# Two of seven block products taken in seven again: a dense graph-layer kernel on one core, with PSUM banks shared anew and a new written order

## The chip, the cores and the metric

The kernel runs on one core of a Trainium2 chip. The metric is the device time of one execution in microseconds (us); before the change its median over 3 runs is 2155.39 us (2154.95 to 2155.68).

## The reference, cut to what matters

Four layers work on x, 128 graphs of 128 nodes with 512 features, in fp32. Each layer adds its result to x and takes a layernorm over the features (no scale, no shift).

```python
# layer 0
y = einsum('nm,bmd->bnd', adj, x);  out = einsum('bnd,do->bno', y, weight) + bias
# layer 1
q = x @ Wq.T;  k = x @ Wk.T;  v = x @ Wv.T
rel = adj.T * (q @ k.T);  rel = rel / norm(rel, axis=2);  out = rel @ v
# layer 2
h = x @ W;  e = leaky_relu(h @ a1 [:, None] + h @ a2 [None, :], 0.2) * adj
out = elu(softmax(e) @ h + beta * h)
# layer 3
A = adj @ x;  C = A + b;  out = max over features of relu(A + (C - A))   # per node
x = layernorm(x + out)   # after each layer
```

The kernel uses that layer 1's scores are x (Wq.T Wk) x.T, that layer 2's aggregation can come before the weight product ((att + beta I) x) W, and that layer 3's sum is A + b.

## The kernel before, in words

The 128 graphs are worked in 32 groups of 4 (`G`, `NG`), so a group is 512 rows. Per group there are four big products of 512 x 512 by 512 x 512, named after their weight: `y` with weight "0" (layer 0), `m` with "m" (x times the combined Wq.T Wk, made once in the fill as product `qk`), `v` with "v", and `z` with "2" (layer 2). Besides these there are, for each of the 4 graphs, small PE pieces: the aggregation `p_y` (with adj), the scores `p_rel`, the attention times values `p_o`, the aggregation `p_z`, and `p_a` of layer 3.

**Seven products.** Each big product is split into 2 x 2 blocks of 256 and taken in Strassen-Winograd form: seven block products instead of eight (`product`, L451), on sums and differences of the weight's blocks (`weight_blocks`, L157, made once) and of the left factor's blocks (`left_factors`, L335, by GpSimd, for every product). A block product is four fp32 matmuls of 128 x 128 weights with 256 columns. They accumulate in three PSUM regions (`REGION`, L332): region 0 collects products 1, 6, 7 and 4, region 1 product 2, region 2 products 5 and 3. After each product, what the region holds by then is brought into its output block (`BLOCK`, L333) by a ScalarE copy or a VectorE addition (`out`, L481). In y the bias is laid into the regions beforehand by ScalarE (`fill`, L457).

In the steady groups (y of groups 2 to 31, m and v of 1 to 30, z of 0 to 29), product 2, which feeds only block (0, 0), is itself taken in seven products of 128-blocks (`inner_product`, L420): its own sums of the left factor are made by GpSimd (`inner_sums`, L354, 128 columns wide), its own sums of the weight once (`inner`, L183), and its seven 128 x 128 x 128 products come in four stretches (`SMALL`, L400) that share one PSUM bank with tag "pi" and are added to the four quarters of the output block by VectorE, seven additions of 128 columns.

**The written order.** Nothing is scheduled by a planner. Every piece of work is put into a list by `emit` with a number, its place in the order (L240); `TABLE` (L252) holds the places for a group, and group g is shifted by 28 g. The list is sorted and emitted (L1141), and each engine works through its own pieces in just that order (`InOrder`, L18). A group spans some 110 units, so four groups are in work at once, each in another layer; a period of 28 units has one group's worth of every piece. Inside a big product the places are in `STEPS` (L408): for each block product when it starts and when its output is taken, and likewise for the inner stretches. `EARLY` and `FIRST` (L273, L281) hold the places of groups 0 and 1, `LAST` (L289) those of the last three groups. In the fill the order of the products is y of group 0, qk, m of group 0, y of group 1, v of group 0; these are plain (all seven products of 256-blocks, in the order 1, 2, 6, 5, 7, 3, 4).

**Between the layers.** VectorE adds residuals, takes the dots of layer 2 (`dots`, L739), the statistics and the row maxima; ScalarE copies products out of PSUM, squares, exponentiates and applies the normalisations (`apply`); GpSimd makes the left sums and every -1/2 power of a layernorm (`norm`, L522). Transposes of x and of the attention go through VectorE in blocks of 32 and then DMA (`turn_blocks`, `move`), issued from SyncE.

**PSUM.** The eight banks are: two for all small PE pieces (tag "ps", `bank`, L85), two for region 0 ("r0"), one for regions 1 and 2 ("r12"), one for the inner products ("pi"), and two for the constant vectors of layer 2 ("wa").

```python
ORDER = (1, 2, 6, 5, 7, 3, 4)
REGION = {1: 0, 6: 0, 7: 0, 4: 0, 2: 1, 5: 2, 3: 2}
BLOCK = {1: (0, 0), 2: (0, 0), 6: (0, 1), 3: (0, 1), 5: (1, 1), 7: (1, 1), 4: (1, 0)}
```

Of the kernel before, what the change touches and what calls it, by code (L numbers as in the profile page):

```python
# [8 lines left out]
FP = mybir.dt.float32  # L9
AF = mybir.ActivationFunctionType  # L10
ALU = mybir.AluOpType
# [18 lines left out]
def kernel(  # L30
# [41 lines left out]
    G = 4  # L72
# [7 lines left out]
    small = ctx.enter_context(tc.tile_pool(name="small", bufs=4))  # L80
# [51 lines left out]
    for tag, n in (("r0", 2), ("r12", 1)):  # L132
        for i in range(n):
            r = psum.tile([P, 2, H], FP, tag=tag, name=f"first_{tag}_{i}", bufs=n)
            pe.matmul(r, ident, ident[:, None, :].to_broadcast([P, G, P]), start=True, stop=True)
# [21 lines left out]
    def weight_blocks(at, key, w, keep=0, tag=None):  # L157

# [7 lines left out]
        def factor(i):  # L166
            if i == 0:
                home, args = (const, {}) if tag is None else (data, dict(tag=tag))
                u = home.tile([P, 3 + keep, 2, H], FP, name=f"t_{key}", **args)
                t.update({2: u[:, 0], 3: u[:, 1], 4: u[:, 2]})  # L170
                t[1] = u[:, 3] if keep else blk(0, 1)
                bw[key] = {
                    1: blk(0, 0), 2: blk(1, 0), 3: blk(1, 1), 4: t[4], 5: t[1], 6: t[2], 7: t[3],
                }
# [8 lines left out]
        def inner():  # L183

            b = blk(1, 0)
            quad = {(k, c): b[:, k, c * P : (c + 1) * P] for k in range(2) for c in range(2)}
            v = const.tile([P, 4, P], FP, name=f"u_{key}")
# [5 lines left out]
            bw_inner[key] = {  # L193
# [5 lines left out]
        if tag is None:  # L199
            emit(at[3], inner)  # L200
# [46 lines left out]
    def row(at, step, n=G):  # L247
# [3 lines left out]
    YS = 1.3  # L251
    TABLE = dict(  # L252
        load=[-20], y=[0.74, 1.12, 3.36, 3.74], y_sums=[4.5, 5.0, 5.5, 8.0], y_w=row(6.66, 1, 7),
        stats0=[13.7, 14.05, 14.4, 14.7], norm0=[15.15], apply0=row(15.9, 0.33),
        turn=row(21.4, 1), turn_blocks=row(17.3, 0.5),
        move=row(19.3, 0.1), x_sums=row(25.3, 0.5), m=row(28, 1, 7),
        scores=[35.4, 35.78, 38.02, 38.4],
        masked=[38.85], squares=[39.2], turn_rel=[39.1],
        move_rel=row(39.8, 0.1), inverse=[41.0], v=row(41.3, 1, 7),
        attend=[51.12, 52.43, 53.65, 54.02],  # L260
        residual=[51.45, 52.8, 54.0, 54.4], squares1=[51.85, 53.2, 54.35, 54.8],
        dots=[51.75, 53.1, 54.6, 55.6], norm1=[55.9], scale=[57.2],
        apply1=row(65.4, 0.33),
        spread=[57.3], leaky=[61.3], weighted=[62.6], greatest=[63.2], exps=[63.25],
        divide=[64.6], turn_att=[68.6], with_beta=[69.0], turn_blocks_2=[64.95], move_2=[65.0],
        gather=[70.04, 70.42, 72.66, 73.04],
        z_sums=row(73.9, 0.5), z_w=row(76.69, 1, 7), exp=[84.1, 84.9, 96.0, 99.2],
        elu=[85.9, 86.7, 96.85, 99.9], norm2=[101.3], apply2=row(102.3, 0.33),
        widen=[103.95, 104.32, 105.43, 105.81], top=[104.4, 104.95, 105.85, 106.3],
        norm3=[107.3], apply3=row(108.45, 0.33), store=[109.9],  # L270
    )

    EARLY = dict(  # L273
        y=row(0.5, 1), y_sums=row(4.3, 0.5), y_w=row(7, 1, 7),
        stats0=row(14.4, 0.4), norm0=[16.2], m=row(28, 1, 7), scores=row(36.5, 1),
        masked=[39.95], squares=[40.4], turn_rel=[40.3], move_rel=row(41.2, 0.1),
        v=row(42, 1, 7), attend=row(50.6, 1), residual=row(51.0, 1), squares1=row(51.4, 1),
        norm1=[55.5],
# [3 lines left out]
        0: dict(EARLY, stats0=row(15.8, 0.02), norm0=[15.95], apply0=row(18.0, 0.1), turn=row(20.4, 0.3),  # L282
                dots=[57.8, 58.75, 59.9, 60.6], scale=[61.2], spread=[62.0], leaky=[62.3], weighted=[62.9],
                greatest=[64.0], exps=[64.05], divide=[65.05], turn_blocks_2=[65.6], move_2=[65.65]),
        1: dict(y=row(-9.5, 0.3), y_sums=row(-4.0, 0.1), y_w=row(7, 1, 7), stats0=row(14.4, 0.4), norm0=[16.2], attend=[49.7, 52.43, 53.65, 54.02], apply0=row(18.0, 0.1), turn=row(20.3, 0.3),
                x_sums=row(22.5, 0.5)),
# [4 lines left out]
            exp=[0.8, 10.5, 13.0, 18.0], elu=[4.4, 12.3, 17.2, 20.9], norm2=[23.3],  # L291
            apply2=row(24.6, 0.8), squares3=row(28.0, 0.8), widen=[44.7, 54.9, 55.0, 59.3],
            top=[45.6, 58.77, 58.78, 61.05], norm3=[64.32], apply3=row(66.0, 0.8), store=[69.0],
        ),
        NG - 2: dict(
            scale=[4.2], apply1=row(4.5, 0.9), spread=[6.9], leaky=[7.4], weighted=[9.0],
            greatest=[11.5], exps=[12.2], divide=[14.6], turn_att=[18.35], with_beta=[19.6],
            gather=row(33.1, 0.9), z_sums=row(37.0, 0.05),
            z_w=[37.2, 38.9, 41.0, 42.7, 44.9, 46.6, 48.3], exp=[50.3, 51.0, 53.0, 57.0],
            elu=[51.95, 54.2, 58.8, 64.35], norm2=[66.6], apply2=row(67.9, 0.8),  # L300
            widen=[69.3, 70.2, 74.5, 77.3], top=[74.3, 74.9, 76.2, 77.7], stats3=row(75.7, 0.05),
            norm3=[75.95], apply3=row(79.0, 0.8), store=[82.0],
        ),
        NG - 1: dict(
            m=[0.0, 1.73, 3.46, 5.2, 7.4, 9.1, 10.8], scores=row(12.7, 0.9), masked=[16.4],
            squares=[17.2], turn_rel=[20.3], inverse=[19.0],
            v=[16.7, 18.4, 20.6, 22.3, 24.0, 25.8, 27.5],
            attend=row(29.4, 0.86), residual=row(30.4, 0.87), stats1=row(33.9, 0.1),
            norm1=[34.3], dots=row(34.4, 0.1), scale=[42.7], apply1=row(39.0, 0.8),
            spread=[44.0], leaky=[44.1], weighted=[45.6],  # L310
            greatest=[47.0], exps=row(48.0, 0.6), divide=row(48.7, 0.6),
            turn_att=row(49.2, 0.6), with_beta=row(49.7, 0.6), gather=[50.0, 50.9, 55.2, 59.6],
            z_w=[51.8, 56.1, 60.4, 63.9], exp=[55.3, 59.6, 63.9, 67.5],
            elu=[56.5, 62.0, 67.5, 70.9], norm2=[58.75, 64.3, 69.8, 73.2],
            apply2=[60.2, 65.8, 71.3, 74.7], widen=[67.45, 68.4, 73.4, 76.0],
            stats3=[61.1, 66.65, 74.1, 76.5], norm3=[62.0, 67.45, 74.2, 76.6],
            top=[69.86, 73.25, 75.5, 77.0],
            apply3=[70.9, 74.3, 76.4, 78.0], store=[71.8, 75.2, 77.3, 78.9],
# [16 lines left out]
    def left_factors(at, s, aT, tag, name, keep, inner=0):  # L335
# [18 lines left out]
        def inner_sums():  # L354

            a = {
                (j, k): s[aT][:, 2 + k, j * P : (j + 1) * P] for j in range(2) for k in range(2)
            }
            v = work.tile([P, 4, P], FP, tag=tag + "i", name=f"si_{name}")
            s1, s2, s3, s4 = (v[:, i] for i in range(4))  # L360
            pool.tensor_tensor(s1, a[1, 0], a[1, 1], ALU.add)
            pool.tensor_tensor(s2, s1, a[0, 0], ALU.subtract)
            pool.tensor_tensor(s3, a[0, 0], a[1, 0], ALU.subtract)
            pool.tensor_tensor(s4, a[0, 1], s2, ALU.subtract)
            s["fi"] = {1: a[0, 0], 2: a[0, 1], 3: s4, 4: a[1, 1], 5: s1, 6: s2, 7: s3}

        if inner:
            emit(at[2] + inner, inner_sums)
# [14 lines left out]
    def by_columns(p, a, b, first):  # L383

        for c in range(2):
# [15 lines left out]
        ((1, 2), (((0, 0), 1), ((0, 0), 0))),  # L401
        ((6, 5), (((1, 1), 2), ((0, 1), 0))),
        ((7,), (((1, 1), 0),)),
        ((4, 3), (((0, 1), 2), ((1, 0), 0))),
    )


    STEPS = {  # L408
        key: (
            {1: (0.0, 0.45), 6: (1.69, 2.4), 5: (2.62, 3.3), 7: (4.22, 4.9), 3: (5.16, 5.85), 4: (5.91, 6.6)},  # L410
            ((1.5, 1.65), (2.43, 2.6), (4.12, 4.18), (4.97, 5.15)),
        )
        for key in ("m", "0", "v")
    }
    STEPS["2"] = (
        {1: (0.0, 0.6), 6: (1.69, 2.4), 5: (3.0, 3.7), 7: (4.21, 4.9), 3: (5.9, 6.55), 4: (6.64, 7.3)},
        ((1.5, 1.7), (2.81, 2.97), (4.11, 4.2), (5.71, 5.88)),
    )

    def inner_product(at, name, mul, s, w, c):  # L420
# [4 lines left out]
        def step(n):  # L425
            if n == 0:
                q["p"] = psum.tile([P, Q, P], FP, tag="pi", name=f"pi_{name}", bufs=1)
            for i in SMALL[n][0]:
                a, b = s["fi"][i], bw_inner[w][i]
                pe.matmul(  # L430
                    q["p"][:, {2: 1, 5: 2, 3: 2}.get(i, 0), :],
# [7 lines left out]
        def out(n):  # L439
            for (j, h), i in SMALL[n][1]:  # L440
                dst = c(0, 0)
                x, y = (h, j) if columns else (j, h)
                dst = dst[:, x, y * P : (y + 1) * P]
                dve.tensor_tensor(dst, q["p"][:, i, :], dst, ALU.add)
# [727 lines left out]
```

## Time and profile before

| | |
|---|---|
| time | 2155.39 us, median of 3 |
| span of the profiled execution | 2153.9 us |
| one period in the steady part | 65.28 us (a piece at 1001.54 comes again at 1066.82) |
| steady waits of PE for another engine | none in the period shown by the stretches table |
| DVE, ACT, POOL busy in that period | 45.76, 40.52, 27.68 us |
| granted TensorE clock | 1.00 in the period, 0.88 from 2100 us on |
| PE busy from 2100 us to the end | 32.37 of 53.90 us |

PE is TensorE's matmuls, PEld its weight loads, DVE VectorE, ACT ScalarE, POOL GpSimd, SP SyncE. All instructions carry line L26, the helper that keeps them in order, so groups are told apart by their tiles: r_y, r_m, r_v and r_z are the block products of the four big products, pi_y to pi_z the inner ones, s_x and si_x the left sums and the inner left sums. Each fp32 matmul appears as two instructions, so a block product is x8 and a 128-block product x2.[...]

### The profile page before, as it was taken

How to read it: one execution, taken by the hardware profiler on the slowest of the kernel's cores; microseconds unless marked ns; L12 is line 12 of the kernel's file. 1: busy time of each engine (PE TensorE's matmuls, PEld its weight loads, DVE VectorE, ACT ScalarE, POOL GpSimd, SP SyncE). 2: the span in 40 equal slices, each digit the busy share in tenths (PEclk: the TensorE clock that was granted, in tenths of full speed). 3: DMA queues.
4: the chain of work that ended last, by engine and by line, in shares of the span. 5: the costliest groups of instructions: out<-in, count | busy, mean ns of one | idle time of the engine just before them, and what ended most of it. 6: DMA issues, size and time to landing. Idle time of an engine off the chain costs nothing.

```text
span 2153.9 us, 34894 instructions
## 1 busy us (share of the span) xinstructions
PE 2127.1 (99%) x11607; PEld 1827.1 (85%) x11607; DVE 1492.6 (69%) x4105; ACT 1283.9 (60%) x2950; POOL 862.9 (40%) x949
## 2 busy tenths in 40 slices
PE   9999999999999999999999999999999999999995
PEld 7888888888888888888888888888888888888882
DVE  5677776676766676767767767767666767667677
ACT  3346556666556665566665566665567665566654
POOL 4233434343444343344334344434443433443321
PEclk9999999999999999999999999999999999999998
DMA  4012232322232322232221323221323222322201
GB/s 172 25 35 59 60 78 70 74 55 55 65 76 67 72 62 48 71 75 68 55 66 55 76 72 72 54 57 62 77 67 77 56 50 69 76 68 60 50 5 59
DMA packets 361986, 138.49 MB, mean 64 GB/s; under 512 B 303184, under 2 KB 318672, under 8 KB 361808
## 3 DMA queue, kind: packets, MB, share of 16 engines
q1 hardware_dynamic: 361280, 135.22, 24.9%
q8 instruction: 93, 1.52, 0.3%
q10 hardware_dynamic: 528, 1.05, 0.1%
q14 instruction: 85, 0.70, 0.1%
HBM read 55.12 MB, written 41.48 MB: 45 GB/s over the span
## 4 chain that ended last, share of the span: by engine, by line
PE 96%; DVE 2%; ACT 1%; SPq 0%; POOL 0%; issue 0%; DMA 0%; ACTq 0%; POOLq 0%; DVEq 0%
PE r_y L26 16%; PE r_v L26 16%; PE r_m L26 15%; PE r_z L26 14%; PE p_rel L26 5%; PE p_y L26 5%; PE p_z L26 5%; PE p_o L26 5%; PE p_a L26 5%; PE pi_v L26 2%; PE pi_y L26 2%; PE pi_m L26 2%; PE pi_z L26 2%; DVE st L26 1%; SPq L26 0%; ACT x L26 0%
## 5 line engine op out<-in xcount | busy, mean ns | idle before, releaser
L26 ACT ACTIVATE x<-x,nmean,rstd 128x512 f32<-128x512 f32 x384 | 285.4, 807 | 118.1 <-DVE nmean L26 118.0
L26 ACT ACTIVATE scr<-x 128x512 f32<-128x512 f32 x360 | 226.1, 628 | 147.6 <-DVE x L26 142.5
L26 POOL TENSOR_TENSOR rstd<-ve,mhalf 128x4 f32<-128x4 f32 (+1 forms) x99 | 99.1, 1001 | 390.3 <-DVE ve L26 390.0
L26 ACT COPY tT<-r_m 128x512 f32<-128x512 f32 x128 | 74.9, 586 | 238.6 <-PE r_m L26 238.5
L26 DVE TENSOR_TENSOR x<-r_y,x 128x512 f32<-128x512 f32 x194 | 132.5, 683 | 77.2 <-PE r_y L26 72.4
L26 DVE SCALAR_TENSOR_TENSOR scr<-x,wa 128x512 f32<-128x512 f32 x256 | 174.4, 681 | 4.6
L26 DVE TENSOR_REDUCE mx<-p_a 128x1 f32<-128x512 f32 x128 | 88.3, 691 | 117.2 <-PE p_a L26 117.2
L26 POOL TENSOR_TENSOR s_y<-yT 128x512 f32<-128x512 f32 x32 | 40.6, 1268 | 250.6 <-ACT yT L26 250.6
L26 POOL TENSOR_TENSOR rn<-n,mhalf 128x4 f32<-128x4 f32 x32 | 32.6, 1018 | 254.2 <-ACT sq L26 254.2
L26 POOL TENSOR_TENSOR s_x<-xT 128x512 f32<-128x512 f32 x64 | 81.8, 1278 | 128.0 <-DMA xT<-xB 83.1
L26 PEld LDWEIGHTS p_z<-eT,x 128*128 128x128 f32 x1024 | 124.4, 192 | 5.3 <-issue 1.0
L26 PE MATMUL p_a<-x,adjT 128*128 128x512 f32 x256 | 122.6, 600 | 6.2 <-ACT x L26 6.2
L26 PEld LDWEIGHTS p_rel<-xT,tT 128*128 128x128 f32 x1024 | 124.6, 192 | 3.6 <-ACT tT L26 0.2
L26 PEld LDWEIGHTS p_y<-adjT,x 128*128 128x128 f32 x1024 | 124.1, 192 | 3.8 <-ACT yT L26 0.7
L26 ACT COPY v<-r_v 128x512 f32<-128x512 f32 x128 | 74.4, 581 | 88.0 <-PE r_v L26 88.0
L26 PE MATMUL p_o<-v,relT 128*128 128x512 f32 x256 | 125.5, 593 | 0.1
L26 PE MATMUL p_z<-eT,x 128*128 128x128 f32 x1024 | 125.0, 275 | 0.2 <-DVE eT L26 0.2
L26 PE MATMUL p_rel<-xT,tT 128*128 128x128 f32 x1024 | 125.1, 275 | 0.0
L26 PE MATMUL p_y<-adjT,x 128*128 128x128 f32 x1024 | 124.6, 275 | 0.3 <-ACT yT L26 0.3
L26 ACT COPY c<-r_z 128x512 f32<-128x512 f32 x124 | 71.3, 576 | 86.6 <-PE r_z L26 86.6
L26 PE MATMUL r_y<-w_sb,s_y 128*128 128x256 f32 x512 | 121.1, 379 | 0.0
L26 PE MATMUL r_v<-t_v,s_x 128*128 128x256 f32 x512 | 121.1, 379 | 0.0
(218 smaller groups left out, 5676.6 us busy)
## 6 DMA issues: line engine op xcount, KB each, us to landing
out_dram<-x SPq DMA_DIRECT2D x128, 256.0 KB, 2.2
x<-in_x_dram SPq DMA_DIRECT2D x31, 1024.0 KB, 7.6
xT<-xB SPq DMA_DIRECT2D x480, 64.0 KB, 2.3
relT<-relB SPq DMA_DIRECT2D x496, 16.0 KB, 1.8
eBd<-eB SPq DMA_DIRECT2D x30, 256.0 KB, 2.0
eT<-eBd SPq DMA_DIRECT2D x120, 64.0 KB, 2.0
s<-s2d SPq DMA_DIRECT2D x29, 256.0 KB, 5.3
w_sb<-in_L_gnn_weight_dram ACTq DMA_DIRECT2D x1, 1024.0 KB, 6.0
```

What stands on the lines that cost most here:

```text
L26: return lambda *args, **kw: self.tc.keep_in_program_order(op(*args, **kw))
```

## The change

Product 4 of each weight, which feeds only block (1, 0), is now taken in seven products of 128-blocks as product 2 is, in the same 120 products. Five block products and two inner ones remain per big product. It is meant to take multiplications off TensorE.

For that:

- `inner` of `weight_blocks` makes the sums of blocks 2 and 4 of a weight; the fourth plain sum of weights "k" and "2" now overwrites the weight's own block, and the last group, which uses W2 itself, loads it again (`load_again`).
- `inner_sums` works on both halves of the rows at once: the same four GpSimd instructions, 256 columns wide, give the left sums of products 2 and 4. Each has a place of its own in the order (`y_inner`, `x_inner`, `z_inner`).
- An inner product has three stretches instead of four, with four quarters of the bank in use, and seven additions, one of which takes a quarter of the bank twice and is 256 columns wide.
- Product 4 no longer accumulates in region 0. After product 7 that region is put into both blocks (1, 1) and (1, 0); the order is 1, 6, 7, 5, 3, with the stretches of 2 and 4 between, and 5 is added where 7 was.
- Banks: region 0 gets one buffer, the inner products two; region 1 of the plain products uses the inner ones' tag. The first matmul into each bank loses one of three.
- SBUF: the small tiles have two buffers instead of four, e and rel share two, the transposed blocks relB, eB and s2 share two, m has two instead of three.
- All places are new: `TABLE`, `FIRST` (now without `EARLY`), `LAST`, `STEPS` and the places of the weights' preparation.

The diff, cut to its core:

```diff
-    for tag, n in (("r0", 2), ("r12", 1)):
+    for tag, n in (("r0", 1), ("r12", 1)):
...
+        for n, i in enumerate((2, 4)):
+            if inner_at is not None:
+                emit(inner_at[n], inner, i)
...
-        stats0=[13.7, 14.05, 14.4, 14.7], norm0=[15.15], apply0=row(15.9, 0.33),
+        y=[0.4502, 1.7198, 2.5377, 4.2529],
+        stats0=[13.328, 13.6989, 14.9332, 14.6913], norm0=[15.5628],
+        apply0=[17.0291, 17.8869, 17.7334, 18.253], turn=[16.7073, 16.2021, 14.9969, 20.612],
...
+        x_inner=[27.1832, 28.0762, 28.1744, 27.3808],
+        m=[27.6814, 29.311, 30.5193, 32.9685, 32.6007, 32.3909, 36.4113],
...
+        attend=[51.0766, 51.9776, 54.2466, 53.0567], residual=[51.4403, 53.0619, 54.4101, 55.0641],
+        squares1=[51.8389, 54.8288, 55.7527, 55.9297], dots=[52.2629, 53.9621, 54.8819, 55.6838],
+        norm1=[56.0324], scale=[57.2146], apply1=[65.5539, 65.7375, 66.5847, 65.6302],
...
+        move_2=[66.4103], gather=[70.2679, 71.1247, 73.2155, 74.6156],
+        z_sums=[75.1661, 76.1025, 77.0322, 77.3655], z_inner=[76.1384, 77.0913, 77.9699, 79.3217],
+        z_w=[76.5003, 77.2488, 83.0675, 84.5887, 83.8747, 83.1527, 86.1311],
+        exp=[85.3247, 85.2563, 97.2575, 99.4893], elu=[86.3247, 87.0299, 97.3808, 99.5574],
+        norm2=[101.3033], apply2=[101.8904, 102.4013, 101.9063, 102.7223],
...
+                (s["s1"], a[1, 0], ALU.add, a[1, 1]),
+                (s["s2"], s["s1"], ALU.subtract, a[0, 0]),
+                (s["s4"], a[0, 1], ALU.subtract, s["s2"]),
+                (s["s3"], a[0, 0], ALU.subtract, a[1, 0]),
+            )[i]
+            pool.tensor_tensor(to, left, right, op)
...
     SMALL = (
-        ((1, 2), (((0, 0), 1), ((0, 0), 0))),
-        ((6, 5), (((1, 1), 2), ((0, 1), 0))),
-        ((7,), (((1, 1), 0),)),
-        ((4, 3), (((0, 1), 2), ((1, 0), 0))),
+        ((1, 2, 5), (((1, 1), 2), ((0, 0), 1), ((0, 0), 0))),
+        ((6, 3), (((0, 1), 2), ((0, 1), 0))),
+        ((7, 4), (((1, 0), 3), ((1, None), 0))),
     )
+    SMALL_BANK = {1: 0, 6: 0, 7: 0, 2: 1, 5: 2, 3: 2, 4: 3}
...
+        "m": (
+            {
+                1: (0.0547, 0.3858),
+                6: (1.5064, 1.6818),
+                7: (2.8763, 2.9047),
+                5: (4.4211, 5.0801),
+                3: (5.9851, 6.5109),
+            },
+            {
+                2: ((1.231, 1.341), (2.5246, 2.879), (4.1971, 4.3926)),
+                4: ((4.0286, 4.2384), (5.2415, 5.786), (6.8079, 8.6144)),
+            },
+        ),
...
-                q["p"] = psum.tile([P, Q, P], FP, tag="pi", name=f"pi_{name}", bufs=1)
+                q["p"] = psum.tile([P, Q, P], FP, tag="pi", name=f"pi{which}_{name}", bufs=2)
...
+                if h is None:
+                    dst = dst.rearrange("p a (b n) -> p a b n", b=2)
+                    dst = dst[:, :, j, :] if columns else dst[:, j]
+                    src = src[:, None, :].to_broadcast([P, 2, P])
...
+            tag = ("r0", "pi", "r12")[where]
             return psum.tile(
...
+                [P, 2, H], FP, tag=tag, name=f"r{where}_{name}", bufs=2 if tag == "pi" else 1
             )
...
+        def out_inner(i):
+            p = r[REGION[i]]
+            for block in (1, 1), (1, 0):
+                dst = c(*(block if i == 7 else BLOCK[i]))
+                if fresh and REGION[i] == 0:
+                    act.copy(dst, p)
+                else:
+                    dve.tensor_tensor(dst, p, dst, ALU.add)
+                if i != 7:
+                    break
...
-            lead=4.4 if g == 0 else 0.7,
+            lead={0: 4.4, 1: 0.2}.get(g, 0.7),
...
+        def load_again():
+            s["w2"] = data.tile([P, K, D], FP, tag="x1", name="w2_again", bufs=3)
+            sync.dma_start(s["w2"], w2.rearrange("(k p) f -> p k f", p=P))
...
-            s["c", b] = psum.tile([P, D], FP, tag="r0", name=f"c_{g}_{b}", bufs=2)
+            tag = ("r0", "pi")[b % 2]
+            s["c", b] = psum.tile([P, D], FP, tag=tag, name=f"c_{g}_{b}", bufs=1 + b % 2)
...
-            s["m", b] = work.tile([P, D], FP, tag="m", name=f"m_{g}_{b}", bufs=3)
+            s["m", b] = work.tile([P, D], FP, tag="m", name=f"m_{g}_{b}", bufs=2)
```

The places of `LAST` are in units of 1/2.48 from the last group's m on. In them, exp 3 of group 30 comes before elu 2 of group 30, and exp 0 of group 31 between exp 2 and exp 3 of group 30; before, there were three buffers of m for these.

## The prediction, made blind

> **What bounds the kernel now.** I read the page's part 1 and its chain first, then the stretches table for single periods, then the chain in order of time inside one period, then the groups by shape.
>
> ```profile
> PE 2127.1 (99%) x11607; PEld 1827.1 (85%) x11607; DVE 1492.6 (69%) x4105; ACT 1283.9 (60%) x2950; POOL 862.9 (40%) x949
> ...
> PE 96%; DVE 2%; ACT 1%; SPq 0%; POOL 0%; issue 0%; DMA 0%; ACTq 0%; POOLq 0%; DVEq 0%
> ```
>
> PE carries 96% of the chain: what PE issues is the time. The steady part repeats every 65.28 us (the same piece starts at 1001.54 and 1066.82). The stretches table, for that period, gives span, then PE, PEld, DVE, ACT and POOL busy, clock, DMA share, GB/s:
>
> ```profile
> 1001.54:1066.82 65.28, 65.28 (x361) 56.55 (x361) 45.76 (x128) 40.52 (x95) 27.68 (x31) 1.00 0.27 65
> ```
>
> PE has no gap at all, at full clock; DVE has 19.5 us free, ACT 25, POOL 38. Inside it, the chain in order of time (start, length, piece) shows product m:
>
> ```profile
> 1005.00 1.73 PE r_m L26 x8
> 1006.72 1.78 PE p_y L26 x16
> 1008.51 0.45 PE pi_m L26 x4
> 1008.95 1.73 PE r_m L26 x8
> 1010.68 0.45 PE pi_m L26 x4
> 1011.13 1.73 PE r_m L26 x8
> 1012.86 1.78 PE p_y L26 x16
> 1014.64 0.22 PE pi_m L26 x2
> 1014.86 1.73 PE r_m L26 x8
> 1016.59 0.45 PE pi_m L26 x4
> 1017.04 3.46 PE r_m L26 x16
> ```
>
> A 256-block product takes 1.73 us; the one already done in seven 128-block products takes 0.45 + 0.45 + 0.22 + 0.45 = 1.57, by the gaps between starts 1.56. A half of a p_y, p_rel or p_z piece is 0.89, a p_a or p_o 0.86. Check: 24 × 1.73 + 4 × 1.56 + 12 × 0.89 + 8 × 0.86 = 65.3. So the period is nothing but issued matmuls.
>
> **What the skill says, and whether the trace agrees.** "TensorE: Matmul & The Clock Gate", section "Wait — 56ns, not 53.3ns?", puts warm matmuls 55.6 ns apart at 128 columns, N ÷ 2.4 GHz plus 2.5 ns in general; "FP8 and Floating Point Precision", "TensorE Precision Notes", says fp32 takes four passes. Four passes give 0.222 us at 128 columns and 0.437 at 256; the trace has 1.56/7 = 0.223 and 1.73/4 = 0.432. Seven small against eight half-width ones therefore saves 0.17 us, a little less than an eighth. "SBUF — State Buffer", "SBUF: two separate sides", says a DVE instruction with two SBUF inputs and a GpSimd one that reads SBUF lock each other out; here the DVE's e<-s,d takes 1317 ns where e<-p_s,d, from PSUM, takes 692. "PSUM — Partial Sum Buffer", "Specifications (TRN2)", gives eight banks; the kernel's tags use all eight before and after, so a second pi bank must come from r0.
>
> Rows that I price with (groups, mean ns of one; then two instants of the timeline):
>
> ```profile
> L26 DVE TENSOR_TENSOR tT<-pi_m,tT 128x128 f32<-128x128 f32 x210 | 55.1, 286 | 93.2 <-PE pi_m L26 92.1
> L26 POOL TENSOR_TENSOR si_x<-xT 128x128 f32<-128x128 f32 x60 | 27.6, 459 | 0.0
> L26 POOL TENSOR_TENSOR s_x<-xT 128x512 f32<-128x512 f32 x64 | 81.8, 1278 | 128.0 <-DMA xT<-xB 83.1 <-PE p_o L26 17.5 <-DMA out_dram<-x 12.6
> ...
> 995.37 0.48 DVE L26 TENSOR_TENSOR c<-pi_z,c 128x128 f32<-128x128 f32 x2
> 995.77 0.68 DVE L26 SCALAR_TENSOR_TENSOR scr<-x,wa 128x512 f32<-128x512 f32 x1
> ```
>
> Queued DVE work costs less than its mean: two 128-wide adds took 0.40 from start to next start.
>
> **The change, part by part.** (1) *Product 4 in seven.* In y of groups 2 to 31, m and v of 1 to 30, z of 0 to 29, 120 products, one 1.73 becomes 1.56: 0.17 × 120 = **20.4 us** off PE; the period would be 65.28 − 0.68 = 64.60. PE gains 8 → 14 instructions each, 720 in all.
>
> (2) *DVE.* Seven more adds per product, and two of the fourteen are 256 wide. 256 wide is not in the trace: between 0.20 (128) and 0.61 (512, start to start, 1003.54 to 1004.15); I take 0.34. That is 7 × 0.20 + 2 × 0.14 = 1.7 us, 6.7 per period: 45.5 → 52.2 of 64.6 (81%). Free as a total; what matters is who waits behind it. ACT's copies stay four per fresh product (7 is copied twice, 4 no longer; 5 becomes the DVE add that 7 was).
>
> (3) *POOL.* Inner sums are 256 wide, by the line through 0.43 and 1.24 start to start about 0.70, instead of 0.43: 12 × 0.27 = 3.2 us per period, total about 30. It is spread through the written order, so single sums can be late.
>
> (4) *New order.* Each written time modulo 28 gives each engine's sequence. I call the stretches of product 2 2a (small products 1, 2, 5), 2b (6, 3), 2c (7, 4), and those of 4 likewise. I laid the DVE, ACT and POOL pieces along PE's sequence. Most waits clear by 0.5 to 2 us: 2b follows the three adds of 2a (0.6 + 0.2 us) with a 1.73 us product between; r0 is free after product 7's outputs, with 5, 3 and 4b before the next use; p_a's bank waits clear by 2 us. Two do not clear by much.
>
> First: x_inner 1 and 2 now stand on POOL behind the norm1 power, and m's 2b needs them. From p_o2's last matmul: 0.20 to DVE (997.27 to 997.47), then residual 0.67, dots 1.33, adds of 4b 0.40, residual 0.67, out3 0.60, dots 1.33, norm1's small ones 0.85 = 5.85; power 1.09; two sums 1.40. Total 8.54 to the second sum. PE meanwhile has 4b 0.45, P3 1.73, P1 1.73, 4c 0.45, p_y 0.89, 2a 0.67, P6 1.73, p_y 0.89 and the first half of 2b 0.22 = 8.76. Slack 0.2. Queued behind 2b are all PE pieces of the period, so any lateness here is lost entirely.
>
> Second: z's copies sit among the eight normalisations on ACT. From p_z1's end: copy 0.7, exp 0.6, elu's second half 0.8, square 0.6, two copies 1.0, seven normalisations 5.0 (0.71 each), two copies 1.0, then two sums 2.6 and the inner sum 0.7 on POOL: 13.0. PE has 12.9 up to 2a and 0.44 more until the small product that reads that sum: 13.3. Slack 0.3.
>
> These rest on bounded prices (256-wide 0.61 instead of 0.34, sums 0.82 instead of 0.70, the shared-port lock delaying si_x during the small two-input DVE work): the bad ends turn each slack into 0.3 to 0.7 us of wait. I take 0.15 us of wait per period: 30 × 0.15 = **4.5 us** back.
>
> (5) *Banks, in the fill.* r0 has one buffer. The plain products follow each other without PE work between in three places: y_0 to qk and y_1 to v_0 each wait for the last DVE output (0.2 + 0.61 + wake-up, 0.9), m_0 to y_1 for an ACT copy and then the bias fill (0.2 + 0.5 + 0.5 + 0.1, 1.3): 3.1 us. Against that one of three warm-up matmuls goes (5.49/3 = 1.8 us of PE before adjT), of which about 1.0 is kept, since the last quarter of x lands about 6.7 us after its issue near 3.5, and the fill order may save 0.5. Net **+1.5**.
>
> (6) *Drain.* From 2100 on PE is busy 32.4 of 53.9 us; a relay of DVE and ACT sets it. The direct products get three banks for two (they waited 1.2 us once), but m has two buffers for three, so exp 3 of group 30 waits on ACT for elu 2, and ACT's queue with it. I take 0, ±3. Reloading W2 in the last group, sharing SBUF tiles (e with rel, blocks) and two small buffers cost nothing: their previous readers end several us earlier, and DMA share is 0.27. The weights' own sums (8 sets of four 128-wide, about 1 us each) fall in the fill beside PE.
>
> Sum: 2155.4 − 20.4 + 4.5 + 1.5 = **2141 us**.
>
> **Rivals.** *No waits, good ends*: 2155.4 − 20.4 − 2 = 2133; for it, both slacks are positive as worked out; against, they are smaller than their uncertainty. *Gain given back*: a wait of 0.6 to 0.7 each period takes the place of 4's saving, 2153 to 2158; DVE at 81% in order speaks for it. *Slower*: the two near waits add up, or DVE falls behind PE for good in the stretch of residuals and dots, where it is busy without a break for 12 us; 1.2 us per period gives 2155.4 + 30 × (1.2 − 0.68) + 1.5 = 2172. Against it: a period holds only 52 us of DVE work for 64.6 of PE, and each chain starts anew from a PE piece.
>
> **How the numbers follow.** Forecast 0.60, no waits 0.15, given back 0.11, slower 0.14. The first two are faster by over 0.2% (below 2151); the given-back case is mostly within 0.2%: 0.75, 0.10, 0.15. The range 2130 to 2159 leaves out the slower case and a few per cent of better drains.
>
> **What would show it.** Period 64.6 to 64.9 in the chain; pi_ pieces of 0.67 + 0.45 + 0.45 twice per product; DVE near 52 of a period; PE count up by about 720. A wrong step 4 shows as PE waiting before pi_m for POOL si_x, or before pi_z for POOL si_z; wrong step 5 as PE waiting for r_qk, r_y and r_v early on; a period above 65.3 makes the forecast wrong.

## The result, and the profile after

The changed kernel takes 2172.14 us (median of 4 runs, 2171.99 to 2172.45), the kernel before 2155.33 (2154.95 to 2155.68) beside it: a ratio of 1.0078, 95% interval 1.0061 to 1.0096. It is slower; the forecast was 2141, with 2130 to 2159 as its range. Here are part 1 and the chain on the page of the kernel after:

```profile
PE 2123.9 (98%) x12325; PEld 1838.2 (85%) x12325; DVE 1784.4 (82%) x4961; ACT 1289.7 (59%) x2950; POOL 971.8 (45%) x949
...
PE 78%; DVE 9%; POOL 9%; issue 2%; ACT 1%; DMA 0%; SPq 0%; DVEq 0%; POOLq 0%; ACTq 0%
```

PE has 718 instructions more than before, as it should, and no more busy time (2123.9 us for 2127.1). But the chain that was 96% PE now runs through DVE and POOL for 18% of the span: something in each period waits. The stretches table for one period (span, then PE, PEld, DVE, ACT and POOL busy):

```profile
967.20:1033.01 65.81, 65.18 (x386) 56.91 (x385) 55.00 (x156) 40.73 (x94) 30.76 (x31) 1.00 0.26 65
```

The period is 65.82 us over 24 periods, where it was 65.28 and 64.60 was forecast. I count PE's time from one start to the next, since a matmul is shown longer than it holds up the next one: the two first small products of y are shown as 0.61 us, and where nothing waits the next starts 0.45 after them. By these starts 1.17 us of the period is waiting (0.57, 0.56 and a few hundredths), which leaves 64.65 for the matmuls. The waits view of the kernel after names the waits (us in total, times, longest):

```profile
PE pi_y L26 <- DVE x L26: 9.7, 29, 0.3
PE pi_y L26 <- POOL si_y L26: 8.9, 29, 0.4
```

Both come once a period, in product y. The view counts only from where the piece before is shown to end, so its waits are too short; by the starts, 2c (the last stretch of product 2, behind the adds x<-pi_y) loses 0.56 us in the period from 967.20 and 2a's third small product (behind si_y) 0.57. The timeline of the period that begins at 1033 shows how they come about (start, length, engine, piece, and in brackets the idle time before it):

```profile
1031.66 1.27 POOL L26 TENSOR_TENSOR s_y<-yT 128x512 f32<-128x512 f32 x1 [7.60 <-ACT yT L26]
1031.98 1.81 DVE L26 TENSOR_TENSOR e<-s,d 128x512 f32<-128x512 f32 x1
1033.01 1.86 POOL L26 TENSOR_TENSOR s_y<-s_y,yT 128x512 f32<-128x512 f32 x1
1033.82 1.60 DVE L26 SCALAR_TENSOR_TENSOR e<-e 128x512 f32<-128x512 f32 x1
1034.83 1.18 POOL L26 TENSOR_TENSOR si_y<-yT 128x256 f32<-128x256 f32 x1
1036.06 0.49 PE L26 MATMUL pi_y<-u,si_y 128*128 128x128 f32 x2 [0.31 <-POOL si_y L26]
1036.09 0.73 POOL L26 TENSOR_TENSOR si_y<-si_y,yT 128x256 f32<-128x256 f32 x1
1038.08 0.69 DVE L26 TENSOR_REDUCE nm<-e 128x4 f32<-128x512 f32 x1 [1.46 <-POOL e L26]
1040.86 1.82 DVE L26 SCALAR_TENSOR_TENSOR e<-e,rs,beta_i 128x128 f32<-128x128 f32 x4
1043.39 0.60 DVE L26 TENSOR_TENSOR x<-pi_y,x 128x128 f32<-128x128 f32 x2
1044.15 0.68 PE L26 MATMUL pi_y<-u,yT 128*128 128x128 f32 x4 [0.35 <-DVE x L26]
```

Two sums on POOL of the same shape, both s_y, take 1.27 us in the first row, where POOL started first, and 1.86 in the third, where DVE's leaky (e<-s,d and e<-e) is under way; the first inner sum takes 1.18, the next, after leaky has ended, 0.73. DVE is longer too: e<-e takes 1.60 here and 0.69 in group 0 (at 115.20), where no GpSimd instruction runs beside it. So each holds up the other; I call this the lock. PE waits for that first inner sum. From there the lateness goes through weighted (POOL's e<-e,adj_sb) to greatest (the row maxima nm, behind 1.46 us of idle DVE), to the exponentials, to divide, which is 1.82 long, to the turn eB, and behind them all to the two adds x<-pi_y for which 2c waits.

The whole difference adds up, by the first starts of the z products: the first r_z comes at 145.57 instead of 140.02 (fill +5.5); from there 29 periods to the product z of group 29 take 15.6 more (2053.39 − 145.57 against 2032.24 − 140.02), 0.54 each; the rest takes 116.85 instead of 121.68 (−4.8). That is +16.3, and the spans differ by 2170.2 − 2153.9 = 16.3.

### The profile page after: what moved, and what is told of

Same layout as the page of the kernel before. It is cut to its first block, busy times and chain, and to the rows that moved or that the text cites. A ratio compares the mean times of both kernels' runs of the same rounds, so it can differ in the third digit from the quotient of the medians.

```text
span 2170.2 us, 36980 instructions
## 1 busy us (share of the span) xinstructions
PE 2123.9 (98%) x12325; PEld 1838.2 (85%) x12325; DVE 1784.4 (82%) x4961; ACT 1289.7 (59%) x2950; POOL 971.8 (45%) x949
## 3 DMA queue, kind: packets, MB, share of 16 engines
q10 hardware_dynamic: 528, 1.05, 0.1%
## 4 chain that ended last, share of the span: by engine, by line
PE 78%; DVE 9%; POOL 9%; issue 2%; ACT 1%; DMA 0%; SPq 0%; DVEq 0%; POOLq 0%; ACTq 0%
PE r_v L26 13%; PE r_z L26 12%; PE r_m L26 10%; PE r_y L26 6%; PE p_z L26 5%; PE p_y L26 5%; PE p_o L26 5%; PE p_a L26 5%; PE pi_v L26 4%; POOL s_y L26 4%; PE pi_z L26 4%; PE pi_m L26 3%; DVE x L26 3%; POOL si_y L26 3%; PE pi_y L26 2%
## 5 line engine op out<-in xcount | busy, mean ns | idle before, releaser
L26 DVE TENSOR_TENSOR tT<-pi_m,tT 128x128 f32<-128x128 f32 x420 | 121.2, 306 | 54.3 <-PE pi_m L26 47.8
L26 PE MATMUL p_a<-x,adjT 128*128 128x512 f32 x256 | 131.8, 601 | 5.9 <-ACT x L26 4.2
L26 PEld LDWEIGHTS p_z<-eT,x 128*128 128x128 f32 x1024 | 131.6, 192 | 6.5 <-DVE x L26 0.8
L26 PE MATMUL p_y<-adjT,x 128*128 128x128 f32 x1024 | 134.5, 275 | 0.4 <-DMA x<-in_x_dram 0.4
L26 PE MATMUL p_z<-eT,x 128*128 128x128 f32 x1024 | 134.8, 275 | 0.0
L26 ACT COPY yT<-p_y 128x512 f32<-128x512 f32 x128 | 74.9, 585 | 100.2 <-PE p_y L26 100.2
L26 DVE TENSOR_TENSOR c<-pi_z,c 128x128 f32<-128x128 f32 x420 | 124.0, 307 | 11.3 <-PE pi_z L26 2.4
L26 PE MATMUL p_o<-v,relT 128*128 128x512 f32 x256 | 130.7, 595 | 0.3 <-ACT xT L26 0.2
L26 DVE TENSOR_TENSOR x<-pi_y,x 128x128 f32<-128x128 f32 x420 | 120.8, 306 | 9.4
L26 DVE TENSOR_TENSOR v<-pi_v,v 128x128 f32<-128x128 f32 x420 | 119.2, 302 | 6.2
```

Source lines behind the costliest of these rows:

```text
L26: return lambda *args, **kw: self.tc.keep_in_program_order(op(*args, **kw))
```

## The experiments

The theory to test, A: leaky and POOL's sums hold each other up, the written order has put them side by side, and both waits of PE come from it. Rivals: B, DVE has too much work in all (55.0 of 65.8 us); C, the one buffer of region 0 costs time in each period. Kernels 1 and 5 were run once; the runs of one kernel differ by up to 1.8 us.

| kernel | time, us (before in the same session) | ratio to before, 95% | period, us |
|---|---|---|---|
| after | 2172.14 (2155.33) | 1.0078 (1.0061 to 1.0096) | 65.82 |
| 1 leaky's operand from PSUM | 2141.86, one run (2155.48) | | 64.77 |
| 2 POOL order | 2169.36 (2155.48) | 1.0066 (1.0051 to 1.0081) | 65.69 |
| 3 DVE order | 2167.78 (2155.48) | 1.0058 (1.0043 to 1.0073) | 65.66 |
| 4 both orders | 2154.14 (2155.48) | 0.9994 (0.9985 to 1.0003) | 65.17 |
| 5 as 1, DVE as long as in after | 2144.88, one run (2155.15) | | 64.88 |
| 6 whole leaky through PSUM, alternating | 2153.41 (2155.15) | 0.9991 (0.9983 to 0.9999) | 65.18 |
| 7 as 6, fill banks exchanged | 2150.75 (2155.15) | 0.9979 (0.9970 to 0.9987) | 65.17 |
| 8 as 6, both orders | 2167.80 (2155.15) | 1.0058 (1.0045 to 1.0072) | 65.66 |
| 9 whole leaky through PSUM, grouped | 2143.05 (2155.37) | 0.9942 (0.9930 to 0.9955) | 64.84 |
| 10 as 9, fill banks exchanged | 2140.72 (2155.37) | 0.9932 (0.9919 to 0.9946) | 64.80 |
| 11 as 10, bias of y_1 earlier | 2139.26 (2155.37) | 0.9924 (0.9912 to 0.9937) | 64.81 |

**1. Leaky's operand from PSUM.**

```diff
+            other = s["s2"] if late or g == 0 else wa[:, 0, :].rearrange("p (b n) -> p b n", b=G)
             dve.tensor_tensor(
                 e,
-                s["s2"],
+                other,
...
-            dve.scalar_tensor_tensor(e, e, ALPHA, e, op0=ALU.mult, op1=ALU.max)
+            last = e if late or g == 0 else other
+            dve.scalar_tensor_tensor(e, e, ALPHA, last, op0=ALU.mult, op1=ALU.max)
```

> The two operations of leaky on DVE (e<-s,d and e<-e) take the row dots as their second operand in place of the scores that the DMA brought, so one of the two inputs lies in PSUM; the right layer-2 scores are left out of this kernel, and no instruction is added or removed. Theory A (the period is longer because GpSimd's s_y and si_y sums and DVE's leaky, with two SBUF inputs each, hold each other up): the second s_y falls from 1.86 to 1.27 us and the first si_y from 1.18 to 0.73, leaky from 3.4 to about 1.4, PE's wait for si_y (0.57 a period) goes, and the period falls from 65.82 to 65.0 to 65.3; what is left is the wait for DVE's adds x<-pi_y. Rival B (DVE has too much to do in all): leaky is 2 us shorter, but the sums stay as long as they are; PE waits as before or somewhat less, period above 65.5. Rival C (one buffer of r0 costs the time in each period): no change, 65.8.

This kernel leaves out the right layer-2 scores. The period fell to 64.77 and the time by 30 us. From its timeline:

```profile
953.42 0.68 DVE L26 TENSOR_TENSOR e<-wa,d 128x512 f32<-128x512 f32 x1
954.45 1.27 POOL L26 TENSOR_TENSOR s_y<-s_y,yT 128x512 f32<-128x512 f32 x1
955.68 0.73 POOL L26 TENSOR_TENSOR si_y<-yT 128x256 f32<-128x256 f32 x1
957.03 0.39 PE L26 MATMUL pi_y<-u,si_y 128*128 128x128 f32 x2
```

The sums are back at 1.27 and 0.73, and PE starts the small product with no wait. More than expected: of the second wait only about 0.1 us is left, though divide still takes 1.82 us, so its cause was mostly the late start of that relay, not divide. C is refuted for the period: the one buffer is still in place, and the period is 0.12 us above the 64.65 of PE's own work. B is not yet, since leaky is also 2 us shorter here.

**5. The same with DVE kept busy.** To part A from B, the add is made four times.

```diff
+            for again in range(0 if late or g == 0 else 3):
+                dve.tensor_tensor(
+                    e, other, s12[g][:, 0, :, None].to_broadcast([P, G, P]), ALU.add
+                )
```

> As the kernel with leaky's second operand from PSUM (right layer-2 scores left out again), but the add is done four times instead of once, so that DVE works on leaky for as long as in the kernel after: 5 x 0.69 = 3.4 us. It separates the lock from DVE's load. Theory A (the lock alone): GpSimd's sums keep 1.27 and 0.73, the period stays at 64.7 to 64.9, time 2140 to 2144. Rival B (the 2 us less of DVE work were what helped): PE waits again for x<-pi_y or si_y, period 65.5 or more, time 2160 to 2172.

The stretches table for a period of this kernel, and the rows of its timeline that answer to those of after:

```profile
955.57:1020.45 64.88, 64.88 (x386) 56.88 (x385) 55.02 (x159) 40.74 (x94) 29.79 (x30) 1.00 0.27 67
```

```profile
954.58 0.68 DVE L26 TENSOR_TENSOR e<-wa,d 128x512 f32<-128x512 f32 x1
955.61 1.27 POOL L26 TENSOR_TENSOR s_y<-s_y,yT 128x512 f32<-128x512 f32 x1
956.01 2.14 DVE L26 TENSOR_TENSOR e<-wa,d 128x512 f32<-128x512 f32 x3
956.84 0.73 POOL L26 TENSOR_TENSOR si_y<-yT 128x256 f32<-128x256 f32 x1
```

DVE is busy 55.02 us, as in after (55.00), and works on leaky's place for 3.5 us from 0.32 us after the first sum's start, as in after; what is missing is the second SBUF operand (and again the right scores). The waits view shows no steady wait of PE, and POOL is busy 1 us less (29.79 for 30.76). The time is 0.9 us above the expected range, the period within it. So it is the lock and not DVE's load; B is refuted as the cause of this loss.

**2, 3, 4. Only the written order.** First POOL's, then DVE's, then both:

```diff
-        y_sums=[5.3577, 5.4124, 7.8235, 8.8388], y_inner=[6.5498, 7.664, 8.3588, 9.0762],
+        y_sums=[5.3577, 5.4124, 7.8235, 8.8388], y_inner=[5.4, 7.664, 8.3588, 9.0762],
```

> One place in the written order changes: on GpSimd the first inner sum si_y stands before the second s_y instead of behind it. Theory A: the lock stays (one of the two sums is still long), but the first inner sum is done about 1 us earlier than PE needs it, so PE's wait of 0.57 us for si_y goes; the other wait, for x<-pi_y, stays near 0.5. Period 65.2 to 65.35, time about 2172 - 29 x 0.55 = 2156. Rival B: the lateness moves elsewhere, the wait for x<-pi_y grows by what the other loses, time 2170 or more. Rival C: no change.

The wait for si_y went and the one for the adds grew from 0.56 to 0.91 a period; of 16 us expected 3 came. In the waits view of this kernel only the second is left, and it is longer:

```profile
PE pi_y L26 <- DVE x L26: 19.7, 29, 0.7
```

That the lateness moves on is what rival B had said of this run (the time came 0.6 us under its figure). The lock now stretches other sums, and the relay over weighted, greatest and divide is as late as it was.

```diff
-        spread=[58.597], leaky=[61.9353], weighted=[63.694], greatest=[63.7], exps=[64.3087],
-        divide=[64.7559], turn_att=[67.1344], with_beta=[64.8337], turn_blocks_2=[64.9823],
+        spread=[58.597], leaky=[61.9353], weighted=[63.694], greatest=[64.3], exps=[64.3087],
+        divide=[65.62], turn_att=[67.1344], with_beta=[64.8337], turn_blocks_2=[65.65],
```

> Three places in DVE's written order change: greatest stands behind the first adds x<-pi_y, divide and the turn eB behind the second adds x<-pi_y, instead of ahead of them. Theory A: 2c of product y no longer waits for these adds (0.56 us a period), the wait for si_y (0.57) stays, period 65.2 to 65.4, time about 2172 - 29 x 0.55 = 2156. If DVE's work in all is the limit (B), greatest and divide push their lateness on to eB, the transfer of eT and the p_z pieces: period unchanged within 0.2. Rival C: no change.

Here the wait for the adds went, the one for si_y stayed, and a new one came: product 3 of y waits for the output of product 5 (x<-r_y), which now stands behind divide and eB. In the period from 965.01 it is 0.41 us. The period is 0.16 us shorter, so the numbers again fall where rival B had put them.

> The edits of the two kernels before together. Theory A: both waits go, PE has no wait in the period and its work is 64.60 us: period 64.6 to 64.8, time 2172 - 29 x (1.0 to 1.2) = 2137 to 2143, faster than the kernel before. Rival B (DVE is busy 55 us of a period, and its lateness finds another reader): at most half of it is won, 2153 or more. Rival C (the bank r0 with one buffer): no change, 2172.

Both old waits are gone, the new one is there in every period. From the waits view of this kernel:

```profile
PE r_y L26 <- DVE x L26: 7.4, 30, 0.7
```

By the starts it is about 0.5 us a period. The time comes level with the kernel before, but 11 us short of what was expected, and this too is within rival B's figures. So the three orders do not speak against B; experiments 5 and 9 do. In these orders each changed place made another piece late; the two together are worth 18 us and the lock 30. An order that moves leaky itself away from the sums was not tried.

**6, 8. The whole computation without the lock.** Leaky is written so that no DVE instruction has two SBUF tensors: with d as a scalar of each partition, one instruction writes 0.2 (s + d) to a PSUM bank of tag "ps" and a second takes max(s + d, that bank).

```diff
+            if not late and g > 0:
+                w = bank(f"e_{g}").rearrange("p (b n) -> p b n", b=G)
+                for b in range(G):
+                    d, s2 = s12[g][:, 0, b : b + 1], s["s2"][:, b, :]
+                    dve.tensor_scalar(w[:, b, :], s2, d, ALPHA, op0=ALU.add, op1=ALU.mult)
+                    dve.scalar_tensor_tensor(
+                        e[:, b, :], s2, d, w[:, b, :], op0=ALU.add, op1=ALU.max
+                    )
+                s["e"] = e
+                return
```

> The whole computation, with leaky written so that no DVE instruction has two SBUF tensors: for each of the four blocks a tensor_scalar writes ALPHA x (s + d) to a free PSUM bank, and a second instruction takes the larger of s + d (d as a scalar for each partition) and that bank. Eight 128-wide instructions at 0.20 to 0.25, 1.6 to 2.0 us, in place of two of 3.4 us in the kernel after. Theory A: GpSimd's sums at 1.27 and 0.73, no wait in product y, period 64.7 to 64.9, time 2140 to 2145, faster than the kernel before by 0.5 to 0.7%. If a scalar for each partition locks GpSimd too, or the borrowed bank makes p_rel wait: 2150 or more. Rival B (DVE's work in all): a gain in proportion to the 1.5 us saved, at most half of the 1.2 us a period, 2155 or more.

POOL's sums are at 1.27 and 0.73 again, but the period is 65.18. The timeline says why (the first two of the eight instructions, then what follows them):

```profile
958.28 0.44 DVE L26 TENSOR_SCALAR e<-s,d 128x128 f32<-128x128 f32 x1
958.76 0.45 DVE L26 SCALAR_TENSOR_TENSOR e<-s,d,e 128x128 f32<-128x128 f32 x1
...
962.04 0.68 DVE L26 TENSOR_TENSOR tT<-r_m,tT 128x512 f32<-128x512 f32 x1
962.12 1.36 PE L26 MATMUL p_rel<-xT,tT 128*128 128x128 f32 x8
```

The eight instructions come 0.48 us apart, not 0.20 to 0.25: leaky lasts 3.8 us, longer than under the lock, and the add tT<-r_m behind it starts only as p_rel wants to read it, which costs PE about 0.5 us. The lock was not at fault here; the price of the replacement was.

> The leaky through PSUM and the changed written order (first si_y ahead of the second s_y; greatest, divide and eB behind the adds) together. Theory A: with the lock gone the written order is no longer short anywhere, so it adds nothing: within 1.5 us of the kernel with the PSUM leaky alone. If the order was a cause of its own: 2 us or more faster than that.

This expectation failed too: 14 us slower than 6 alone. The changed order adds its own wait (product 3 for x<-r_y, 0.41 in the period from 965.55) to that in p_rel (about 0.5), and with the lock gone there is nothing for it to cure.

**9. Grouped.** The four first instructions now come ahead of the four second ones.

```diff
-                for b in range(G):
-                    d, s2 = s12[g][:, 0, b : b + 1], s["s2"][:, b, :]
-                    dve.tensor_scalar(w[:, b, :], s2, d, ALPHA, op0=ALU.add, op1=ALU.mult)
+                d, s2 = s12[g][:, 0, :], s["s2"]
+                for b in range(G):
+                    dve.tensor_scalar(
+                        w[:, b, :], s2[:, b, :], d[:, b : b + 1], ALPHA, op0=ALU.add, op1=ALU.mult
+                    )
+                for b in range(G):
                     dve.scalar_tensor_tensor(
```

> As the whole computation with leaky through PSUM, but the four tensor_scalar come first and the four second instructions after them, so that no instruction reads what the one just ahead of it wrote (the alternating form took 0.48 us from start to start, 3.8 us in all, and its add tT<-r_m came late for p_rel). Theory A with this addition (no lock, and DVE gives leaky no more time than before): eight at 0.20 to 0.25 from start to start, 1.6 to 2.0 us; no wait in product y or before p_rel; period 64.75 to 64.9, time 2141 to 2145, 0.5 to 0.65% faster than before. If 0.45 us is what such a 128-wide instruction takes in any order: no change from 2153.

```profile
953.78 1.91 DVE L26 TENSOR_SCALAR e<-s,d 128x128 f32<-128x128 f32 x4
954.81 1.27 POOL L26 TENSOR_TENSOR s_y<-s_y,yT 128x512 f32<-128x512 f32 x1
955.72 1.50 DVE L26 SCALAR_TENSOR_TENSOR e<-s,d,e 128x128 f32<-128x128 f32 x4
956.04 0.73 POOL L26 TENSOR_TENSOR si_y<-yT 128x256 f32<-128x256 f32 x1
```

The time was as expected, 2143; the prices were not: the first kind stays at 0.48 apart, the second falls to 0.36, so leaky takes 3.4 us, as long as in after. That 0.4 us less than in 6 is enough for p_rel, so the time was met by luck and not by the prices expected. With DVE busy 1782.8 us on its page, against 1784.4 in after, the kernel is 29 us faster: once more the lock and not the load, this time with nothing left out.

**7, 10, 11. The fill.** In qk, m_0 and v_0 the first two regions exchange their banks, so that none of them waits for the only buffer of r0; in 11 the bias of y_1 is also laid into its bank earlier.

```diff
             tag = ("r0", "pi", "r12")[where]
+            if name in ("qk", "m_0", "v_0"):
+                tag = ("pi", "r0", "r12")[where]
...
-            lead={0: 4.4, 1: 0.2}.get(g, 0.7),
+            lead={0: 4.4, 1: 2.0}.get(g, 0.7),
```

> The same, and in the fill the products qk, m_0 and v_0 take their first bank from the tag pi (two buffers) and their second from r0, the other way round, so that none of them waits for the only buffer of r0. If the one buffer of r0 is what the fill lost: y_0 to qk 1.0, m_0 to y_1 1.5 and y_1 to v_0 1.0 us of PE waiting go, and the time falls by 2.5 to 3.5 us against the kernel with the PSUM leaky alone. If these waits only moved ahead of others (sums, weights from HBM): by 0 to 1 us.

> The same with the banks of qk, m_0 and v_0 exchanged in the fill. Theory: the fill's part is independent of the period's, so another 2.3 to 3 us less: 2138 to 2142.

> The same, and in the fill the bias of y_1 is copied into its bank 2 slots ahead of the product instead of 0.2, which the exchanged banks allow. If the remaining wait of 1.3 us between m_0 and y_1 is that copy's place on ACT behind m_0's last copies: another 0.8 to 1.3 us less, 2137 to 2141. If the bank itself is late: no change.

The exchange moves the first r_z from 145.40 to 143.13 in 7 (the same from 9 to 10: 145.36 to 143.04), the earlier bias in 11 on to 141.70: 2.3 and 1.3 us, and the times follow (−2.7, −2.3, −1.5). So 3.6 us of the fill go with the exchanged banks and the earlier bias that they allow. These edits do not touch the period; what the single buffer of r0 costs there, experiment 1 has shown. Kernel 11 beats both kernels: 0.76% under before. On its page the chain is back at 96% PE, with 3% DVE and no POOL.

## Why the prediction was wrong, point by point

- **Step 1, 0.68 us of PE per period: right.** In kernels 1, 5 and 9 to 11, without the lock under leaky and without a late p_rel, the period is 64.77 to 64.88, against 64.60 forecast and 65.28 before; what is left is short waits of 0.1 to 0.2 us. PE has 718 instructions more, 720 were forecast.
- **Step 2, DVE: the size was off, the reading right.** 55.0 us per period instead of 52.2 (which starts from 45.5, where the line shows 45.76); three adds in a row take 0.72 from start to next start, 0.24 each and not 0.20, and divide and leaky are longer. Experiment 5 shows that the load as a total costs nothing, as step 2 said.
- **Step 3, inner sums of 0.70: right where nothing lies beside them** (0.73). That "single sums can be late" was the point that mattered, and it was not followed up.
- **Step 4, the new order: this is the step that failed**, in its sentence "Most waits clear by 0.5 to 2 us". It was right on the two waits that it named as near: m's 2b lost 0.03 us in the period from 967.20 and z's 2a nothing. (The 5.85 in the sum for the first leaves out its 0.20; the total of 8.54 has it.) Product y's 2a and 2c, which it does not name, fall among those declared clear, priced as if nothing lay beside their sums, and lost 0.57 and 0.56. The lock stood in the prediction, from the Trainium skill's page "SBUF — State Buffer", section "SBUF: two separate sides", which says that the one that starts first has the port for its whole instruction and the other is blocked. But it was applied to si_x and the small DVE operations only, not to s_y and si_y under leaky, two DVE instructions of 512 columns. The trace agrees with the page: +0.59 on the second s_y, +0.45 on the first si_y, and leaky at 3.41 us, where its two instructions take 0.68 and 0.69 with an operand from PSUM. The 0.15 us taken for all waits should have been 1.17: 29 periods of 1.02 us more are 29.6 of the 31 us by which the forecast missed, and steps 5 and 6 nearly cancel.

What could have been seen: the trace of before has the same collision, at a place where it did no harm. First come two rows of its groups of instructions (busy us, mean ns of one), then its timeline:

```profile
L26 POOL TENSOR_TENSOR yT<-yT 128x512 f32<-128x512 f32 x32 | 61.4, 1917 | 0.0
L26 POOL TENSOR_TENSOR s_y<-s_y,yT 128x512 f32<-128x512 f32 x32 | 40.7, 1271 | 2.5
```

```profile
1016.89 1.27 POOL L26 TENSOR_TENSOR s_y<-s_y,yT 128x512 f32<-128x512 f32 x1
1017.70 1.31 DVE L26 TENSOR_TENSOR e<-s,d 128x512 f32<-128x512 f32 x1
1018.12 1.99 POOL L26 TENSOR_TENSOR yT<-yT 128x512 f32<-128x512 f32 x1
1019.05 1.60 DVE L26 SCALAR_TENSOR_TENSOR e<-e 128x512 f32<-128x512 f32 x1
```

There leaky starts 2.2 us after the first s_y, and the third sum takes the stretch (1.99 for 1.27), which PE has no need of yet; the inner sums come from 1021.96 on, after leaky. In the new order leaky starts 0.3 us after the first s_y, and the stretch falls on the two sums that PE waits for next. A row of 1917 ns beside one of 1271 for the same shape asked why; the prediction priced all such sums by the short row.

- **Step 5, the fill: +5.5 instead of +1.5 (its own terms give 1.6).** The three waits for r0 were right: 1.04, 0.95 and 1.46 us by PE's starts, 3.45 in all for 3.1 forecast; experiments 7, 10 and 11 win 3.6 there. What was missed is the written order of the fill, taken as half a microsecond of gain: waits of 0.85 (product 4 of y_0 behind a DVE add), 1.05 (the same in m_0) and 1.46 (p_s for DVE's d near 113) are new. The first two were not looked into further. In the third most is the lock again: a DVE instruction of only eight columns, with two SBUF tensors, lasts until the sum beside it has ended.

```profile
112.38 1.26 POOL L26 TENSOR_TENSOR s_y<-s_y,yT 128x512 f32<-128x512 f32 x1
112.56 1.10 DVE L26 TENSOR_TENSOR d<-d,rstd 128x8 f32<-128x8 f32 x1
113.81 0.62 PE L26 MATMUL p_s<-ident,d 128*128 128x128 f32 x4 [1.30 <-DVE d L26]
```

In the kernel before it took 0.31 us at this place, and 0.17 where GpSimd was idle. Rewriting leaky does not touch this wait; the waits view of kernel 11 still has it.
- **Step 6, the drain: −4.8, forecast 0 ± 3.** From the first r_z of group 30 to the end it is 62.2 us for 67.6. The wait of 1.39 us between the direct products is gone, as the prediction's third bank suggested; the rest is not taken apart here.
- **The rivals.** "Slower" had the time almost exactly, 2172 by 1.2 us of wait per period, but by luck, since it meant other waits: its two near chains hold, and DVE does not fall behind in the stretch of residuals and dots.

## What to carry to other kernels

An order written out by hand places instructions beside each other, and where a DVE instruction with two SBUF tensors met GpSimd sums here, the one that started second got longer: take the lengths from instances that lie as the new order puts them, not from means, and look in the old trace for the longest instance of each form. If the two must meet, write the DVE one with one operand in PSUM; that was worth 29 us here, where the changes of places that were tried were worth at most 18, and each made another piece late. A bank with one buffer cost time here only where products follow each other with no other PE work between.

## What the runs showed of the hardware that was not expected

- DVE instructions of one SBUF tensor with a scalar for each partition, 128 columns wide, come 0.48 us apart when they write to PSUM, and 0.36 with a second tensor from PSUM (0.48 where each depends on the one ahead of it), while the plain adds from PSUM of the same width come 0.24 apart.
- These forms leave GpSimd's sums at 1.27 and 0.73 us: one SBUF tensor on DVE does not slow them, two of 512 columns made them 1.86 and 1.18.
- A DVE instruction of 8 columns with two SBUF tensors takes 0.17 us where GpSimd is idle and 1.10 where it starts 0.18 us after a GpSimd sum of 512 columns, which keeps its 1.26: how small it is does not help it.
- The four instructions of divide, each with two SBUF tensors, take 1.82 us beside GpSimd sums and 1.14 where GpSimd is idle (experiment 3).
